# Whitening of a local-attention output: the 128x128 block-diagonal matrices become stacked 64x64 blocks

## The chip, the cores and the metric

The kernel runs on one core of a Trainium2 chip. Its engines work side by side, each through its own queue: TensorE (PE, matrix products; its weight loads are listed as PEld), VectorE (DVE), ScalarE (ACT), GpSimd (POOL), and the DMA queues, most of them issued by SyncE (SP). The metric is the time of one execution in device microseconds (us); lower is better.

## What is computed

The input x has 4 images of 256 channels of 64x64 pixels. The first layer is a local attention: a 7x7 convolution with dilation 2 and a 1x1 convolution give 49 logits for each pixel, a softmax turns them into weights, and each output pixel is the weighted sum of 49 shifted pixels of x. The second layer whitens the result in groups of 64 channels (4 groups; m is 4 x 64 x 64 pixels):

```python
x = jnp.transpose(X, (1, 0, 2, 3)).reshape(g, nc, -1)     # g = 4 groups, nc = 64
mean = x.mean(-1, keepdims=True)
xc = x - mean
Sigma = EPS * I + jnp.einsum('gdm,gem->gde', xc, xc) / m
rTr = (1.0 / jnp.einsum('gii->g', Sigma))[:, None, None]
Sigma_N = Sigma * rTr
P = I
for _ in range(T_ITERS):                                  # 5
    P3 = jnp.einsum('gij,gjk,gkl->gil', P, P, P)
    P = 1.5 * P - 0.5 * jnp.einsum('gij,gjk->gik', P3, Sigma_N)
wm = P * jnp.sqrt(rTr)
xn = jnp.einsum('gde,gem->gdm', wm, xc)                   # then * weight + bias
```

## The kernel before

All data are fp32. The 256 channels are two chunks (cc = 0, 1) of 128 partitions, so each chunk holds two whitening groups of 64 channels (GW = 64), one in partitions 0 to 63, one in 64 to 127.

The long first part, to about 674 us, is convolution and attention. While attention blocks finish, L1093 transposes them, L1101 copies them out and L1114 adds up the moments in the PSUM tile `sig`: for each chunk a 128x65 block whose rows 0 to 63 hold the first group's 64x64 second moments and whose rows 64 to 127 the second group's, with the channel sums in column 64.

Then comes whitening, a Python generator `whiten(cc)` per chunk; the two are stepped in turn, so their instructions alternate. Nothing else is left to do in this time but the output stage, which needs the result. Its steps, by line:

- Head. L1304 makes the mean `mu` from `sig`. L1306 scales the identity by it (`D`), and the product L1308 with `blk`, a 128x128 matrix of ones within each group, spreads the means over rows. L1310 negates mu. L1313 fills S with EPS times the identity (scheduled early, near 579 us), L1317 adds each group's second moments into its diagonal block, one instruction per group, and L1320 subtracts the product of the means. L1320 leaves a nonzero only where `blk` has ones, so S is 128x128 with two 64x64 blocks and zeros elsewhere. L1323 and L1325 take the diagonal of S (`dg`); the product L1327 with `blk` sums it to the trace; L1330 is its reciprocal `rtr`; L1331 scales S; L1335 and L1337 make the first iterate Pm = 1.5 I - 0.5 S. Pm and S lie side by side in the tile `PS`.
- Four iterations. L1342 multiplies Pm with [Pm, S], 256 columns, into PSUM; L1300 evicts the result to `sq` (on ACT for chunk 0, on DVE for chunk 1); L1349 multiplies its two halves (128 columns); L1350 scales Pm by 1.5; L1352 subtracts half the product.
- End. L1357 to L1363 make the output scale from the trace. L1367 multiplies Pm with mu; L1370 and L1371 make the shift; L1376 swaps scale and shift between the two groups' partitions and L1378 copies them out (`abx`).

The matrices are symmetric, and zeros outside the two blocks are carried through every product.

The output stage then applies the matrices: L1429 multiplies a full 128x128 matrix with 512 columns, L1445 multiplies the two diagonal 64x64 blocks (`wm[cc][i, i]`) with 512 columns in quarters of the array, L1396 (ACT) and L1398 (DVE) scale and shift into `out` tiles, and L1433 stores them. Its order on TensorE is kept as written (`pe(...)`); elsewhere a scheduler orders the instructions by priority and data. Semaphores follow from data.

PSUM tiles: `tp()` gives one of three rotating banks; `cv_buf` are two banks that the convolution uses until shortly before the end and that the output stage takes in turn with `apply`.

Of the kernel before, what the change touches and what calls it, by code (L numbers as in the profile page):

```python
# [9 lines left out]
F32 = mybir.dt.float32  # L10
AF = mybir.ActivationFunctionType
ALU = mybir.AluOpType
# [20 lines left out]
def kernel(  # L33
# [29 lines left out]
    nc = tc.nc  # L63
    B, C, H, W = x.shape
    P = 128
    NCC = C // P
# [8 lines left out]
    NPIX = B * H * W  # L75
    GW = 64
    T_ITERS = 5
    EPS = 1e-5
# [24 lines left out]
    def tp():  # L103
        return ps_tp.tile([P, 512], F32, tag="tp", name="tp")


    ident = const.tile([P, P], F32, name="ident")
# [44 lines left out]
    t = tp()  # L152
# [3 lines left out]
    t = tp()  # L156
# [4 lines left out]
    cv_buf = []  # L161
    for k in range(2):
        t = ps_cv.tile([P, 512], F32, name=f"cv{k}")
# [50 lines left out]
    def evict(k, o, i):  # L214
        (nc.vector.tensor_copy if k % 2 else nc.scalar.copy)(o, i)

    for k, c0 in enumerate(range(0, P, CB)):
        n = min(CB, P - c0)
        t = cv_buf[k % 2]
        for cc in range(NCC):  # L220
# [5 lines left out]
                    start=True, stop=True,  # L226
# [8 lines left out]
    for k0 in range(0, KT, TB):  # L235
        n = min(TB, KT - k0)
        t = tp()
# [235 lines left out]
    def col_ops(src, i):  # L473

        X = src.rearrange("p q r c (b a two) -> p (q r c b) a two", a=4, two=2)
        s3 = lambda v: v.rearrange("p (e b) two -> p e b two", b=Q8)
        X4 = [s3(X[:, :, a]) for a in range(4)]
        o = {
            b: xh[b][:, :Q8].rearrange("p q e b two -> p (q e) b two")[:, :, :Q8] for b in ORDER
        }  # L480
        E, O = s3(ct[:, :, 0:2]), s3(ct[:, :, 2:4])
        EO = ct.rearrange("p e (a two) -> p e a two", a=2)
        if i == 0:
            add(EO, X[:, :, 0:2], X[:, :, 2:4])
            yield
            add(o[1], E, O)
            sub(o[2], E, O)
            nc.scalar.copy(o[0], X4[0])
        elif i == 1:
            madd(EO, X[:, :, 2:4], 4.0, X[:, :, 0:2])  # L490
            yield
            madd(o[3], O, 2.0, E)
            madd(o[4], O, -2.0, E)
            nc.scalar.copy(o[INF], X4[3])  # L494
        else:
            madd(o[5], X4[0], 2.0, X4[1])
            yield
            madd(o[5], o[5], 2.0, X4[2])
            yield
            madd(o[5], o[5], 2.0, X4[3])  # L500
# [286 lines left out]
    gs = [col_ops(xr, i) for i in three]  # L787
# [65 lines left out]
    bpool = ctx.enter_context(tc.tile_pool(name="bp", bufs=1, side="right"))  # L853
# [8 lines left out]
    for k in range(NY):  # L862
        a = bpool.tile([P, NCC, P // GW, GW + 1], F32, name=f"yt{k}")
# [95 lines left out]
    back = []  # L959
# [26 lines left out]
    def load_band(n, part):  # L986
# [4 lines left out]
        m0, m1 = BAND[part]  # L991
        D = sd[n % 2][:]
        for g in range(CR):
            dma = nc.sync.dma_start(
                band[g * SW : (g + 1) * SW, m0:m1, g : g + KS].rearrange("p m e w -> p m (e w)"),
                bass.AP(
                    tensor=D.tensor,
                    offset=D.offset + g * SW * DW + m0 * KS * SW + R,
                    ap=[[DW - 1, SW], [KS * SW, m1 - m0], [1, KS * SW]],
# [271 lines left out]
    rpool = ctx.enter_context(tc.tile_pool(name="rp", bufs=1, reuse_waits="tile"))  # L1271
# [6 lines left out]
    blk = rpool.tile([P, P], F32, name="blk")  # L1278
# [9 lines left out]
    finish()  # L1288


    def square(name):
        return bpool.tile([P, P], F32, tag="xb", name=name, bufs=4)

    wm, sc, beta, abx = {}, {}, {}, {}

    def whiten(cc):


        def evict(o, i):
            (nc.vector.tensor_copy if cc else nc.scalar.copy)(o, i)  # L1300

        G = sig[:, cc]
        mu = work.tile([P, 1], F32, tag="mu", name=f"mu{cc}")
        nc.vector.tensor_scalar(mu, G[:, GW : GW + 1], 1.0 / NPIX, None, ALU.mult)  # L1304
        D = square(f"D{cc}")
        nc.vector.tensor_scalar(D, ident, mu, None, ALU.mult)  # L1306
        t = tp()
        nc.tensor.matmul(t[:, :P], blk, D, start=True, stop=True)  # L1308
        nmu = work.tile([P, 1], F32, tag="nmu", name=f"nmu{cc}")
        nc.vector.tensor_scalar(nmu, mu, -1.0, None, ALU.mult)  # L1310
        PS = rpool.tile([P, 2, P], F32, tag="PS", name=f"PS{cc}", bufs=2)
        S = PS[:, 1]
        nc.vector.tensor_scalar(S, ident, EPS, None, ALU.mult)  # L1313
        yield
        for g in range(P // GW):
            gs = slice(g * GW, (g + 1) * GW)
            nc.vector.scalar_tensor_tensor(  # L1317
                S[gs, gs], G[gs, :GW], 1.0 / NPIX, S[gs, gs], ALU.mult, ALU.add
            )
        nc.vector.scalar_tensor_tensor(S, t[:, :P], nmu, S, ALU.mult, ALU.add)  # L1320
        yield
        dt_ = square(f"dt{cc}")
        nc.vector.tensor_tensor(dt_, S, ident, ALU.mult)  # L1323
        dg = work.tile([P, 1], F32, tag="dg", name=f"dg{cc}")
        nc.vector.tensor_reduce(dg, dt_, AX.X, ALU.add)  # L1325
        t = tp()
        nc.tensor.matmul(t[:, :1], blk, dg, start=True, stop=True)  # L1327
        yield
        rtr = work.tile([P, 1], F32, tag="rtr", name=f"rtr{cc}")
        nc.vector.reciprocal(rtr, t[:, :1])  # L1330
        nc.vector.tensor_scalar(S, S, rtr, None, ALU.mult)  # L1331


        i15 = square(f"i15_{cc}")
        nc.vector.tensor_scalar(i15, ident, 1.5, None, ALU.mult)  # L1335
        Pm = PS[:, 0]
        nc.vector.scalar_tensor_tensor(Pm, S, -0.5, i15, ALU.mult, ALU.add)  # L1337
        yield

        for it in range(1, T_ITERS):  # L1340
            t = tp()
            nc.tensor.matmul(  # L1342
                t[:, : 2 * P], Pm, PS.rearrange("p a c -> p (a c)"), start=True, stop=True
            )
            sq = rpool.tile([P, 2, P], F32, tag="sq", name=f"sq{cc}_{it}", bufs=2)
            evict(sq.rearrange("p a c -> p (a c)"), t[:, : 2 * P])
            yield
            t = tp()
            nc.tensor.matmul(t[:, :P], sq[:, 0], sq[:, 1], start=True, stop=True)  # L1349
            nc.vector.tensor_scalar(Pm, Pm, 1.5, None, ALU.mult)  # L1350
            yield
            nc.vector.scalar_tensor_tensor(Pm, t[:, :P], -0.5, Pm, ALU.mult, ALU.add)  # L1352
            yield


        q = work.tile([P, 1], F32, tag="q", name=f"q{cc}")
        nc.scalar.activation(q, rtr, AF.Sqrt)  # L1357
        qi = work.tile([P, 1], F32, tag="qi", name=f"qi{cc}")
        nc.vector.reciprocal(qi, q)
        nc.vector.scalar_tensor_tensor(q, qi, rtr, q, ALU.mult, ALU.add)  # L1360
        ab = work.tile([P, 2], F32, tag="ab", name=f"ab{cc}")
        scale = ab[:, 0:1]
        nc.vector.scalar_tensor_tensor(  # L1363
            scale, q, 0.5, gain_sb[:, cc : cc + 1], ALU.mult, ALU.mult
        )
        t = tp()
        nc.tensor.matmul(t[:, :1], Pm, mu, start=True, stop=True)  # L1367
        yield
        bt = ab[:, 1:2]
        nc.vector.tensor_scalar(bt, t[:, :1], scale, -1.0, ALU.mult, ALU.mult)  # L1370
        nc.vector.tensor_tensor(bt, bt, shift_sb[:, cc : cc + 1], ALU.add)  # L1371
        wm[cc], sc[cc], beta[cc] = Pm, scale, bt
        yield

        t = tp()
        nc.tensor.matmul(t[:, :2], swap, ab, start=True, stop=True)  # L1376
        abx[cc] = work.tile([P, 2], F32, tag="abx", name=f"abx{cc}")
        nc.vector.tensor_copy(abx[cc], t[:, :2])  # L1378

    chains = [whiten(cc) for cc in range(NCC)]  # L1380
    for _ in itertools.zip_longest(*chains):
        pass
# [17 lines left out]
    def two_banks():  # L1400
        while True:
            t = ps_y.tile([P, 2, NT], F32, tag="y", name="apply")
            yield [t[:, k] for k in range(2)]
            yield cv_buf

    G0, G1 = slice(0, GW), slice(GW, P)
    two = two_banks()
    for b in (3, 2, 1, 0):
        for cc in range(NCC):
            for q in range(0, SH // TR, 2):  # L1410
# [30 lines left out]
                for k in range(2):  # L1441
                    for i in (G0, G1):
                        o = i if k == 0 else (G1 if i is G0 else G0)
# [3 lines left out]
                                start=True, stop=True, skip_group_check=True,  # L1447
# [41 lines left out]
```

## Time and profile before

| | us |
|---|---|
| three runs | 745.64, 747.56, 749.41 (median 747.56) |
| the profiled execution | 746.19 |
| span of its instructions | 744.4 |
| mean granted TensorE clock | 0.986 of full speed |

| engine | busy us | share of the span | instructions |
|---|---|---|---|
| PE | 703.4 | 94% | 7512 |
| DVE | 611.3 | 82% | 1268 |
| ACT | 332.5 | 45% | 953 |
| POOL | 51.6 | 7% | 52 |

How to read it: a product of fp32 operands appears as two weight loads and two matmul records, so x4 stands for two products. Ends of matmuls are modelled, so PE counts as busy while it only waits for a result to leave the array; whether it bounds a stretch is seen from what the next engine waits for. "[0.25 <-PE tp L1342]" behind a row says how long its engine stood idle before it and which instruction ended that. A shape 128*64 128x65 is a product with 128 rows and 64 columns of weights and a 128x65 result. PEclk is the TensorE clock that was granted, 1.00 being full speed.

### The profile page before, as it was taken

What the parts mean: (1) busy time and instruction counts of PE and PEld (TensorE: products, weight loads), DVE (VectorE), ACT (ScalarE), POOL (GpSimd) and SP (SyncE); (2) the same over time, 40 slices, a digit from 0 to 9 for tenths busy, and PEclk for the clock granted to TensorE, in tenths of its full rate; (3) what the DMA queues carried; (4) which work ended last, traced back from release to release, by engine and by line L of the source; (5) the groups of instructions that cost most, each with busy time, mean ns of one, the idle gap of its engine ahead of it and who ended that gap; (6) DMA issues with size and microseconds to landing.
All of it is one profiled execution on the core that took longest, in us unless ns stands there. A gap on an engine that the chain in (4) does not pass through costs nothing.

```text
span 744.4 us, 18491 instructions
## 1 busy us (share of the span) xinstructions
PE 703.4 (94%) x7512; PEld 528.3 (71%) x7512; DVE 611.3 (82%) x1268; ACT 332.5 (45%) x953; POOL 51.6 (7%) x52
## 2 busy tenths in 40 slices
PE   6999999997999897999999999999999889998996
PEld 1449543377898794799998958898998678885331
DVE  3789998999999989968995999799969655535575
ACT  1424240255364543466444435735535663322564
POOL 0410070020001110001000100000000000000000
PEclk9999999999899999999999999999999999999999
DMA  8991120147263491076545820534423144371588
GB/s 319 250 319 73 60 88 12 60 147 212 87 193 112 146 317 48 21 245 199 185 128 201 253 69 7 166 108 135 155 64 95 32 149 118 104 296 72 219 357 327
DMA packets 59629, 114.41 MB, mean 154 GB/s; under 512 B 22887, under 2 KB 42008, under 8 KB 58776
## 3 DMA queue, kind: packets, MB, share of 16 engines
q1 hardware_dynamic: 55848, 94.36, 38.7%
q0 software_dynamic: 3696, 18.88, 7.3%
q8 instruction: 59, 0.97, 0.5%
q14 instruction: 26, 0.21, 0.1%
HBM read 65.88 MB, written 47.33 MB: 152 GB/s over the span
## 4 chain that ended last, share of the span: by engine, by line
PE 61%; DVE 28%; ACT 4%; issue 3%; DMA 2%; SPq 0%; DVEq 0%; ACTq 0%
PE cv L538 20%; PE y L1061 12%; PE acc L685 6%; PE tp L1429 4%; PE tp L1093 3%; PE sig L1114 3%; PE cv L685 3%; PE tp L1032 3%; DVE xh L313 3%; DVE pv L313 3%; DVE zz L313 2%; DVE rb L313 2%; PE cv L222 2%; DVE ct L313 2%; DVE band L1009 2%
## 5 line engine op out<-in xcount | busy, mean ns | idle before, releaser
L538 PE MATMUL cv<-xh,wr 128*49 128x128 f32 x4368 | 250.2, 276 | 5.7 <-DVE rm L899 5.3
L538 PEld LDWEIGHTS cv<-xh,wr 128*49 128x49 f32 x4368 | 244.1, 124 | 9.6 <-ACT xh L494 5.5
L1061 PE MATMUL y<-band,xb 128*128 128x224 f32 (+2 forms) x640 | 150.6, 373 | 7.6 <-ACT xb L1040 5.9
L1061 PEld LDWEIGHTS y<-band,xb 128*128 128x128 f32 x640 | 109.1, 192 | 29.0 <-ACT xb L1040 8.9
L548 ACT COPY pv<-cv 113x486 f32<-113x486 f32 (+1 forms) x63 | 30.0, 476 | 86.1 <-PE cv L538 85.8
L1080 ACT ACTIVATE slot<-y,pivot 128x512 f32<-128x512 f32 x53 | 36.6, 738 | 63.5 <-PE y L1061 63.4
L1101 ACT COPY yt<-tp 128x256 f32<-128x256 f32 x128 | 45.6, 378 | 38.8 <-PE tp L1093 37.6
L1032 PE MATMUL tp<-ident,slot 128*128 128x128 f32 x256 | 49.9, 297 | 6.7 <-ACT yt L1101 6.7
L313 DVE SCALAR_TENSOR_TENSOR pv<-pv 113x162 f32<-113x162 f32 x186 | 54.9, 318 | 1.0 <-ACT pv L548 0.4
L1093 PE MATMUL tp<-ident,slot 128*128 128x128 f32 x256 | 52.1, 299 | 3.6 <-ACT yt L1101 1.0
L1009 DVE STREAM_TRANSPOSE band<-band 128x864 f32<-128x864 f32 (+1 forms) x48 | 47.4, 990 | 9.5 <-DMA band<-sd 9.5
L1093 PEld LDWEIGHTS tp<-ident,slot 128*128 128x128 f32 x256 | 41.3, 205 | 13.8 <-issue 4.4
L1032 PEld LDWEIGHTS tp<-ident,slot 128*128 128x128 f32 x256 | 39.9, 205 | 13.0 <-ACT yt L1101 8.0
L941 ACT COPY zt<-d 32x112 f32<-32x112 f32 (+2 forms) x156 | 44.8, 287 | 1.9
L893 ACT ACTIVATE d<-tp,mx 128x49 f32<-128x49 f32 x128 | 37.0, 336 | 17.4 <-DVE mx L888 13.9
L313 DVE SCALAR_TENSOR_TENSOR xh<-ct 128x512 f32<-128x512 f32 x42 | 27.8, 683 | 14.1 <-PE cv L538 13.7
L1114 PE MATMUL sig<-yt 128*64 128x65 f32 x1024 | 36.9, 225 | 0.0
L1114 PEld LDWEIGHTS sig<-yt 128*64 128x64 f32 x1024 | 32.4, 137 | 6.0 <-issue 4.5
L1040 ACT COPY xb<-tp 128x256 f32<-128x256 f32 x87 | 30.5, 376 | 12.9 <-PE tp L1032 12.4
L1040 DVE COPY xb<-tp 128x256 f32<-128x256 f32 x41 | 16.5, 421 | 23.5 <-PE tp L1032 23.5
L685 PE MATMUL acc<-slot,tap 128*49 128x496 f32 (+3 forms) x168 | 34.6, 569 | 0.0
L893 ACT ACTIVATION_READ_ACCUMULATOR d<-tp,mx 128x1 f32 x128 | 30.6, 241 | 0.0
(222 smaller groups left out, 959.2 us busy)
## 6 DMA issues: line engine op xcount, KB each, us to landing
out_dram<-out SPq DMA_DIRECT2D x32, 512.0 KB, 3.4
sd<-zt SPq DMA_DIRECT2D x16, 896.0 KB, 4.2
slot<-in_x_dram POOLq DMA_DIRECT2D x12, 1024.0 KB, 10.0
band<-sd SPq DMA_DIRECT2D x128, 84.0 KB, 2.2
wr<-gd SPq DMA_DIRECT2D x15, 588.0 KB, 3.7
wr<-gd SPq DMA_DIRECT2D x15, 490.0 KB, 3.9
spill<-slot POOLq DMA_DIRECT2D x3, 2048.0 KB, 7.7
back<-spill SPq DMA_DIRECT2D x3, 2048.0 KB, 13.3
```

The lines of the kernel that those rows point to most:

```text
L313: return in_turn(STT(o, a, f, b, ALU.mult, ALU.add))
L538: nc.tensor.matmul(cv[h * HB : h * HB + KT, k, sr : sr + n, sc : sc + n], wv[:, sc, sr, cc], xh[bc][:, :n, h * NCC + cc, :n], start=(j == ...
L685: nc.tensor.matmul(ps[h * HB : h * HB + KT, :, w0:w1_], w[v][:, cc], xs[:, :, cc, w0 + d : w1_ + d], start=(j == 0), stop=(j == len(order) ...
L893: nc.scalar.activation(d[:, h, i], lt[i // NI][:, i % NI, h, :KT], AF.Exp, bias=mx[:, i, h : h + 1], accum_out=s[:, h, i : i + 1],)
L941: ins = nc.scalar.copy(o, i)
L1009: return nc.vector.transpose(f, f)
L1032: nc.tensor.transpose(t[:, cc * P : (cc + 1) * P], xt[:, cc, CR * m : CR * (m + 1), bass.ds(pc, SW, 2)], ident,)
L1040: (nc.vector.tensor_copy if tail else nc.scalar.copy)(xb, t[:, :C])
L1061: nc.tensor.matmul(ps[:, cc, q0 - half * HALF : q1 - half * HALF, :], xb[:, cc * P : (cc + 1) * P], rhs, start=(k == 0), stop=(k == len(PI ...
L1093: nc.tensor.transpose(t[:, cc * P : (cc + 1) * P], yt[:, cc, CR * i : CR * (i + 1), bass.ds(pc, SW, 2)], ident,)
L1101: nc.scalar.copy(yb.rearrange("p a g c -> p (a g) c")[:, :, :GW], t[:, :C].rearrange("p (e c) -> p e c", c=GW),)
L1114: nc.tensor.matmul(sig[g * GW : (g + 1) * GW, cc], yb[:, cc, g, :GW], yb[:, cc, g], start=(count[0] == 0 and cc == 0), stop=(count[0] == 4 ...
```

## The change

The whitening matrices lose their zeros. Each chunk's Pm, S and what goes with them become 128x64 tiles: the first group's 64x64 block in partitions 0 to 63, the second's in 64 to 127. `own` is the identity in that form, `eps` and `i15` are multiples of it, made once.

Each product of the iterations becomes two products of 64x64 weights (`parts_mm`), one per group, in different quarters of the array; for chunk 1 the squares are written to the other half of the partitions (`crossed`) and the second products write them back, so that the two chunks use different quarters. The diagonal for the trace is taken from `sig` directly, with the mean's square subtracted from the sums, and its product with `blk` is issued next to the mean's product, into a bank of `cv_buf`. At the end the two blocks of Pm are copied into a zeroed 128x128 matrix `full[cc]`, which the product with mu and the output stage use. In the changed kernel's own line numbers: L1322 is the eviction and the copy to `full`, L1314 every product of `parts_mm`, L1330 and L1341 the products with `blk`, L1345 and L1346 build S, L1349 the reciprocal, L1354 the first Pm, L1365 and L1367 the update, L1384 the product with mu, L1387 and L1388 the shift, L1393 the swap, L1445 and L1461 the output products.

```diff
-    def square(name):
-        return bpool.tile([P, P], F32, tag="xb", name=name, bufs=4)
+    G0, G1 = slice(0, GW), slice(GW, P)
+
+    def small(name):
+        return rpool.tile([P, GW], F32, name=name)
+
+    own, eps, i15 = small("own"), small("eps"), small("i15")
+    nc.vector.tensor_tensor(own, ident[:, :GW], ident[:, GW:], ALU.add)
+    nc.vector.tensor_scalar(eps, own, EPS, None, ALU.mult)
+    nc.vector.tensor_scalar(i15, own, 1.5, None, ALU.mult)
+    full = []
+    for cc in range(NCC):
+        full.append(rpool.tile([P, P], F32, name=f"full{cc}"))
+        nc.gpsimd.memset(full[cc], 0.0)
+
+    def parts_mm(t, lhs, rhs, crossed, back=False):
+        for i, o in ((G0, G1 if crossed else G0), (G1, G0 if crossed else G1)):
+            if back:
+                i, o = o, i
+            nc.tensor.matmul(
+                t[o], lhs[i], rhs[i], start=True, stop=True, skip_group_check=True
+            )
...
-        D = square(f"D{cc}")
-        nc.vector.tensor_scalar(D, ident, mu, None, ALU.mult)
+        D = small(f"D{cc}")
+        nc.vector.tensor_scalar(D, own, mu, None, ALU.mult)
         t = tp()
-        nc.tensor.matmul(t[:, :P], blk, D, start=True, stop=True)
+        nc.tensor.matmul(t[:, :GW], blk, D, start=True, stop=True)
...
-        PS = rpool.tile([P, 2, P], F32, tag="PS", name=f"PS{cc}", bufs=2)
-        S = PS[:, 1]
-        nc.vector.tensor_scalar(S, ident, EPS, None, ALU.mult)
-        yield
-        for g in range(P // GW):
-            gs = slice(g * GW, (g + 1) * GW)
-            nc.vector.scalar_tensor_tensor(
-                S[gs, gs], G[gs, :GW], 1.0 / NPIX, S[gs, gs], ALU.mult, ALU.add
-            )
-        nc.vector.scalar_tensor_tensor(S, t[:, :P], nmu, S, ALU.mult, ALU.add)
-        yield
-        dt_ = square(f"dt{cc}")
-        nc.vector.tensor_tensor(dt_, S, ident, ALU.mult)
+        dt_ = small(f"dt{cc}")
+        nc.vector.tensor_tensor(dt_, G[:, :GW], own, ALU.mult)
         dg = work.tile([P, 1], F32, tag="dg", name=f"dg{cc}")
         nc.vector.tensor_reduce(dg, dt_, AX.X, ALU.add)
-        t = tp()
-        nc.tensor.matmul(t[:, :1], blk, dg, start=True, stop=True)
+        nc.vector.tensor_scalar(dg, dg, 1.0 / NPIX, EPS, ALU.mult, ALU.add)
+        nc.vector.scalar_tensor_tensor(dg, mu, nmu, dg, ALU.mult, ALU.add)
+        tt = cv_buf[cc]
+        nc.tensor.matmul(tt[:, :1], blk, dg, start=True, stop=True)
+        PS = rpool.tile([P, 2, GW], F32, tag="PS", name=f"PS{cc}", bufs=2)
+        S = PS[:, 1]
+        yield
+        nc.vector.scalar_tensor_tensor(S, G[:, :GW], 1.0 / NPIX, eps, ALU.mult, ALU.add)
+        nc.vector.scalar_tensor_tensor(S, t[:, :GW], nmu, S, ALU.mult, ALU.add)
         yield
         rtr = work.tile([P, 1], F32, tag="rtr", name=f"rtr{cc}")
-        nc.vector.reciprocal(rtr, t[:, :1])
+        nc.vector.reciprocal(rtr, tt[:, :1])
         nc.vector.tensor_scalar(S, S, rtr, None, ALU.mult)
-        i15 = square(f"i15_{cc}")
-        nc.vector.tensor_scalar(i15, ident, 1.5, None, ALU.mult)
...
         for it in range(1, T_ITERS):
             t = tp()
-            nc.tensor.matmul(
-                t[:, : 2 * P], Pm, PS.rearrange("p a c -> p (a c)"), start=True, stop=True
-            )
-            sq = rpool.tile([P, 2, P], F32, tag="sq", name=f"sq{cc}_{it}", bufs=2)
-            evict(sq.rearrange("p a c -> p (a c)"), t[:, : 2 * P])
+            parts_mm(t[:, : 2 * GW], Pm, PS.rearrange("p a c -> p (a c)"), cc)
+            sq = rpool.tile([P, 2, GW], F32, tag="sq", name=f"sq{cc}_{it}", bufs=2)
+            evict(sq.rearrange("p a c -> p (a c)"), t[:, : 2 * GW])
             yield
             t = tp()
-            nc.tensor.matmul(t[:, :P], sq[:, 0], sq[:, 1], start=True, stop=True)
+            parts_mm(t[:, :GW], sq[:, 0], sq[:, 1], cc, True)
             nc.vector.tensor_scalar(Pm, Pm, 1.5, None, ALU.mult)
             yield
-            nc.vector.scalar_tensor_tensor(Pm, t[:, :P], -0.5, Pm, ALU.mult, ALU.add)
+            nc.vector.scalar_tensor_tensor(Pm, t[:, :GW], -0.5, Pm, ALU.mult, ALU.add)
             yield
...
+        for i in (G0, G1):
+            evict(full[cc][i, i], Pm[i])
         t = tp()
-        nc.tensor.matmul(t[:, :1], Pm, mu, start=True, stop=True)
+        nc.tensor.matmul(t[:, :1], full[cc], mu, start=True, stop=True)
...
-        wm[cc], sc[cc], beta[cc] = Pm, scale, bt
+        wm[cc], sc[cc], beta[cc] = full[cc], scale, bt
```

More of the change, by code (lines that the diff above doesn't have):

```diff
@@ L1404, in two_banks @@
             yield cv_buf
-    G0, G1 = slice(0, GW), slice(GW, P)
     two = two_banks()
```

## The prediction

> **What bounds the kernel now.** I read the chain of waits first, around the one place that the change touches. Columns: start (us), length (us), engine, tile, line.
>
> ```profile
> 673.14 1.11 PE sig L1114 x32
> ...
> 674.27 0.22 DVE mu L1304 x2
> ...
> 678.45 1.22 PE tp L1342 x4
> ...
> 688.29 0.40 PE tp L1367 x2
> ...
> 689.66 1.34 PE tp L1429 x2
> ```
>
> The last moments end at 674.22, the first output product starts at 689.52. These 15.3 us are whitening alone, and nothing else runs. They split into a head (674.27 to 678.45, where DVE prepares), four iterations (to 687.76) and an end (to 689.52). Then TensorE is busy without a gap until 736.24, so whatever whitening loses moves the end by as much.
>
> The timeline of the last iteration, chunk 0 (chunk 1 runs half a step behind; columns as above, then tiles and shapes):
>
> ```profile
> 685.67 1.24 PE L1342 MATMUL tp<-PS 128*128 128x256 f32 x4
> 686.41 0.23 DVE L1350 TENSOR_SCALAR PS<-PS 128x128 f32<-128x128 f32 x1 [0.25 <-PE tp L1342]
> 686.46 0.37 ACT L1300 COPY sq<-tp 128x256 f32<-128x256 f32 x1 [1.72 <-PE tp L1342]
> 686.88 1.03 PE L1349 MATMUL tp<-sq 128*128 128x128 f32 x4
> 687.42 0.28 DVE L1352 SCALAR_TENSOR_TENSOR PS<-tp,PS 128x128 f32<-128x128 f32 x1
> 687.76 0.27 PE L1367 MATMUL tp<-mu,PS 128*128 128x1 f32 x1
> ```
>
> It is a latency chain: square 0.79, eviction 0.42, second product 0.54, update 0.34, together 2.09. L1350 ends long before L1352 needs it.
>
> The table by stretches (us, then busy time and count of PE, PEld, DVE, ACT, POOL, then PEclk, the granted clock):
>
> ```profile
> 673.10:676.52 3.42, 1.83 (x37) 1.53 (x36) 2.12 (x13) 1.69 (x3) 0.00 (x0) 1.00 0.05 19
> 676.52:679.93 3.41, 2.22 (x10) 1.49 (x10) 2.88 (x15) 0.68 (x3) 0.00 (x0) 0.99 0.00 0
> 679.93:683.34 3.41, 3.35 (x11) 2.19 (x9) 2.18 (x13) 0.37 (x1) 0.00 (x0) 0.51 0.00 0
> 686.76:690.17 3.41, 2.83 (x15) 1.93 (x14) 1.93 (x10) 0.07 (x1) 0.00 (x0) 0.99 0.00 0
> 690.17:693.58 3.41, 3.41 (x11) 0.81 (x10) 0.59 (x1) 0.78 (x1) 0.00 (x0) 0.51 0.00 0
> ```
>
> Twice here the clock is halved for 3.41 us, each time right after a stretch with little work. The first costs the iterations 9.31 - 4 x 2.09 = 0.95 us; the second lies in the output stage, where PE is the bound, and costs half of 3.41, 1.7 us. So 2.65 us of the profiled execution are clock.
>
> Last, the timelines of DVE in the head and of PE in the output stage:
>
> ```profile
> 675.14 0.47 DVE L1317 SCALAR_TENSOR_TENSOR PS<-sig,PS 64x64 f32<-64x64 f32 x2
> 675.54 0.33 DVE L1320 SCALAR_TENSOR_TENSOR PS<-tp,nmu,PS 128x128 f32<-128x128 f32 x1
> 675.90 0.23 DVE L1317 SCALAR_TENSOR_TENSOR PS<-sig,PS 64x64 f32<-64x64 f32 x1
> 676.16 0.29 DVE L1323 TENSOR_TENSOR dt<-PS,ident 128x128 f32<-128x128 f32 x1
> ```
>
> ```profile
> 698.02 0.66 PE L1445 MATMUL apply<-slot,PS 64*64 64x512 f32 x4
> ```
>
> L1317 works on half the partitions at a time; around it each row starts only when the one before has ended (675.90 after 675.87, 676.16 after 676.13), while elsewhere rows overlap: 0.07 us from start to start for one column (674.27, 674.34), 0.13 for 64 (674.41, 674.54). And the four quarters of the array run four 64x64 products in the time of one.
>
> **The head: -1.4.** Out go four L1317, two L1335 and full-width forms; in come, for each chunk, a diagonal product of sig itself, two one-column rows for the trace, and one sig row at full height (L1345) for two halves. I walk the changed program's DVE order with those spacings, a dependent row starting 0.03 after its input ends. Lengths: one column 0.15, 64 columns 0.21 (L1317: 0.20 to 0.23), L1346 0.27 (L1320's 0.34 less 64 columns). From mu0 at 0: dt0 0.07, D0 0.20, dg0 0.40, mu1 0.53, dt1 0.60, D1 0.80, dg0 complete 1.08, dg1's reduction 1.07 to 1.28, the two L1345 at 1.20 and 1.40, dg1 complete 1.69. Trace product of chunk 1: 1.73, its reciprocal 0.42 later (L1367 at 688.29 to L1370 at 688.72), 2.15. Behind it in DVE's order wait the scalings of S (2.22, 2.35), then Pm0, 2.48 to 2.69; PE at 2.73, against 4.18 now: -1.45. The other bound: the 22 rows before took 4.12 with lengths that sum to 5.41 (76%); the 23 new lengths sum to 4.4, and 76% of that is 3.4: -0.8. I take -1.4, for the half-height rows that spoil the 76% are gone; at best -1.6.
>
> The trace's products queue on PE behind both mean products; that hides behind DVE's L1346 rows. Without that cover it is 0.2.
>
> **The iterations: 4 x -0.57 = -2.3.** Each product becomes two 64x64 ones.
> - Square, 128 columns for 256: L1349 has 128 columns and takes 0.54. The weights are 64 columns wide (L1445 loads in 130 ns, L1349 in 188), -0.05; ACT starts 0.05 after DVE, +0.05. So 0.54 for 0.79, -0.25. Ends: 0.43 (L1367, one column) and 0.75 (0.54 and the second pair streamed in turn: 256 columns at 0.84 ns, from four 320-column L1061 in 1.08 us, 0.21).
> - Eviction: ACT copies of 256, 162 and 98 columns take 372, 291 and 241 ns, so 128 take some 0.265, -0.11; on DVE -0.13 (425 at 256, 559 at 392).
> - Second product, 64 columns: between 0.37 (L1367 less 0.06 for weights) and 0.51 (0.40 and 128 columns in turn, 0.11). I take 0.40, as quarters overlap at L1445: -0.14.
> - Update: 287 ns at 128 columns, 219 at L1317's 64: -0.07.
> The ends are -0.30 and -0.73 an iteration, -1.2 and -2.9 in all.
>
> **The end: +0.4.** Pm must become a full matrix: two 64x64 copies per chunk. For chunk 0 on ACT (L701, 64 columns: 213 ns) they take 0.5 with handoffs, under chunk 1, which is 0.5 behind. For chunk 1 on DVE they are 0.2 each (L953, 64x112: 214 ns), the second after the first as around L1317: 0.43, and L1384 waits. Behind L1384 on PE are the swap products and the first output product, which need it anyway; DVE's L1387 waits for PE too. Ends +0.25 and +0.6.
>
> **Hidden.** PE turns from full products to 64x64 ones ahead of the first L1314 and back at L1384. In the output stage a group of four full and eight quarter pieces takes 2.94 us (1.92 and 1.02 in the chain of waits), while their columns at 0.84 ns make 1.72 + 0.86 = 2.58: at most 0.18 for each turn. At both new turns PE waits for DVE anyway, so I take nothing; without that cover +0.36. Three 128x64 rows (own, eps, i15) stand where two L1313 stood, at 579.5; DVE then idles 1.29 us until 581.12. Without that gap: 0.1. Two memsets of 0.21 go to POOL after 580.0, where its work ends at 580.6 for the rest of the program. No DMA, no other queue, and no order ahead of 674 changes.
>
> **The clock: -0.7.** Array time, at 0.84 ns a column: 676.52 to 679.93 had 1284 columns, 1.08 us or 32%; 686.76 to 690.17 some 35%; both were followed by half clock. 673.10 to 676.52 had 47% (1.12 of moments, 0.43 of L1308, 0.05) and wasn't. The changed iteration has 0.64 us of array time (768 columns) in 1.52, 42%; the moments' stretch 39%. Both lie between, so the rows don't decide. Ends: no half clock any more, -2.65; or half clock through all four iterations (0.5 each by the row pair 0.79 and 0.54, which grew to 1.26 and 0.81 at half clock, scaled to 0.94 us of product: 2.0 for 0.95), +1.05. I take -0.7, near the middle.
>
> [...]
>
> [...]
>
> **Sum.** -1.4 - 2.3 + 0.4 - 0.7 = -4.0 on the profiled 746.19 gives 742.2. That execution lies 1.37 below the median of the runs, 747.56, so against the median: **743.6**.
>
> **Rivals.**
> - The clock stays up throughout. For: array share above 35%. Against: head and end still have 1 to 2 us without products. -3.3 - 2.65: 741.6.
> - Half clock through all iterations. For: shorter products, 39% in the stretch ahead. Against: at half clock the array share doubles, and 679.93 to 683.34 was followed by full clock. -3.3 + 1.05: 745.3.
> - Slower: the 64x64 pieces run one after another, each with its latency. Four at the shortest L1349 piece, 275 ns, make 1.10 for 0.79; four at L1114's 222 make 0.89 for 0.54: +0.66, less 0.18 for eviction and update, +0.48 an iteration, +1.9 in all; with head and end +0.9: 748.5. It decides from 0.2 us more for each product, instead of less. Against it stands the L1445 row.
>
> **Chances.** Within 0.5% (743.8 to 751.3) is what a measurement of this kernel can't tell from no change, and my forecast is on that edge. Forecast 58% (743.6; its own range 742.2 to 745.0): 34 faster, 24 same. Clock up 16%: all faster. Half clock 21%: 1 faster, 20 same. Serial pieces 5%: 3 same, 2 slower. That is 0.51, 0.47, 0.02. All best ends give 740.7, all worst 747.6; leaving out 2 in 10, 741.2 to 746.4.
>
> **What would show it.** Head: first L1314 some 2.7 us after the first mu. Iterations: 1.5 us from square to square at PEclk 1.00, the pieces of a pair starting together. End: two L1322 copies ahead of L1384. Clock: PEclk in the 3.41 us stretches around whitening. I am wrong if pairs run in turn, if the head is still over 3.4, or if anything ahead of the last L1114 moves.

## The result, and the profile after

The changed kernel took 746.07 us in the median of 12 runs (744.25 to 748.64), the kernel before 747.70 in 12 runs beside it: a ratio of 0.9983, 95% interval 0.9971 to 0.9995. By the ratio it is faster by about 1.3 us. Forecast were 743.6 us, 4.0 less than before. The profiled execution took 747.68 us, with a span of 745.9 and a mean clock of 0.98.

The chain of waits of the changed kernel, at the places that the prediction showed (start, length, engine, tile, line):

```profile
676.03 1.11 PE sig L1114 x32
...
690.51 1.92 PE tp L1445 x2
```

The last moments end some 3 us later than in the profile before, which the prediction had named as a sign of being wrong. The change is not the cause: its only instructions ahead of them stand at 582.4 to 583.8 us (L1301 to L1307), and one and the same row of ACT (L893) starts at 312.73 before and at 315.61 here, already 2.9 us later. This execution had half clock near 251 us, which the profile before had not, and two stretches of it in place of one near 285; a second profile of the kernel before, below, has the same. Only distances are compared below. From the end of the moments to the first output product (690.37) there are 13.24 us, where there were 15.30.

The same by stages (head, iterations, end; us, busy time and count of PE, PEld, DVE, ACT, POOL, then PEclk, DMA share, GB/s):

```profile
677.13:680.22 3.09, 1.37 (x9) 1.15 (x9) 3.04 (x24) 0.87 (x2) 0.00 (x0) 1.00 0.01 5
680.22:687.45 7.23, 6.63 (x64) 4.18 (x64) 4.33 (x25) 1.16 (x5) 0.00 (x0) 0.59 0.01 2
687.45:690.37 2.92, 1.86 (x9) 1.80 (x9) 1.39 (x8) 0.48 (x2) 0.00 (x0) 0.50 0.00 0
```

Before, these were 4.23, 9.31 and 1.76 us at PEclk 1.00, 0.82 and 1.00. Head and iterations are shorter, the end is longer, and PEclk is the column to read: the clock is now halved nearly throughout the iterations and in all of the end.

The timeline of the first iteration, which began at full clock, the starts of the squares that follow, and the copies at the end:

```profile
680.22 0.48 PE L1314 MATMUL tp<-PS 64*64 64x128 f32 x8 [0.80 <-DVE PS L1354]
680.69 0.27 ACT L1322 COPY sq<-tp 128x128 f32<-128x128 f32 x1 [1.01 <-PE tp L1314]
...
681.01 0.74 PE L1314 MATMUL tp<-sq 64*64 64x64 f32 x8 [0.31 <-ACT sq L1322]
...
681.43 0.58 DVE L1367 SCALAR_TENSOR_TENSOR PS<-tp,PS 128x64 f32<-128x64 f32 x2
...
681.70 1.06 PE L1314 MATMUL tp<-PS 64*64 64x128 f32 x8
...
683.62 1.03 PE L1314 MATMUL tp<-PS 64*64 64x128 f32 x8
...
685.54 1.01 PE L1314 MATMUL tp<-PS 64*64 64x128 f32 x8
...
687.49 0.50 ACT L1322 COPY full<-PS 64x64 f32<-64x64 f32 x2 [0.89 <-DVE PS L1367]
687.79 0.39 DVE L1322 COPY full<-PS 64x64 f32<-64x64 f32 x2
688.04 0.93 PEld L1384 LDWEIGHTS tp<-mu,full 128*128 128x128 f32 x4 [0.81 <-ACT full L1322]
```

From square to square the first iteration took 1.48 us (680.22 to 681.70), against 2.09 before; the next two took 1.92 each. A row of eight squares lasts 0.48 us at first and over 1.0 once the clock is halved.

The table by stretches of 3.41 us around whitening, as in the prediction:

```profile
677.86:681.28 3.42, 2.01 (x20) 1.44 (x20) 2.92 (x24) 0.57 (x3) 0.00 (x0) 1.00 0.00 0
681.28:684.69 3.41, 3.32 (x31) 2.01 (x28) 2.09 (x13) 0.53 (x2) 0.00 (x0) 0.52 0.02 5
684.69:688.10 3.41, 2.63 (x25) 1.81 (x25) 2.17 (x11) 0.75 (x3) 0.00 (x0) 0.50 0.00 0
688.10:691.52 3.42, 2.95 (x10) 2.22 (x10) 1.03 (x7) 0.00 (x0) 0.00 (x0) 0.50 0.00 0
691.52:694.93 3.41, 3.41 (x11) 0.80 (x10) 0.52 (x1) 0.78 (x1) 0.00 (x0) 0.50 0.00 0
694.93:698.34 3.41, 3.41 (x14) 1.08 (x13) 1.90 (x3) 2.19 (x3) 0.00 (x0) 0.97 0.37 154
```

Half clock lasts four stretches without a break, 13.65 us. The kernel before had one stretch in the iterations, then full clock, then one in the output stage. Of the 13.65 us, 4.56 lie behind 690.37 in the output stage. There a group of eight L1461 products takes 1.92 us in the chain of waits at half clock (692.42) and 1.02 at full clock (696.65), so their cost is put at half, 2.3 us, an estimate; before it was 1.7. Whitening gained 2.06, the output stage lost 0.57: 1.5 us, near the 1.3 measured.

So each profile is summed up here by one figure: whitening plus half of the half-clock time in the output stage. It is 17.0 before and 15.5 after. In the further profiles it is counted to the first output product of the chain of waits (690.51 above) and not to its first record (690.37), which adds up to 0.14 us.

### The profile page after: what moved, and what is told of

It reads as the page before. It is cut to its first block, busy times and chain, and to the rows that moved or that the text cites. A ratio compares the mean times of both kernels' runs of the same rounds, so it can differ in the third digit from the quotient of the medians.

```text
span 745.9 us, 18571 instructions
## 1 busy us (share of the span) xinstructions
PE 704.8 (94%) x7544; PEld 529.3 (71%) x7544; DVE 609.9 (82%) x1271; ACT 332.0 (45%) x955; POOL 50.8 (7%) x54
## 4 chain that ended last, share of the span: by engine, by line
PE 66%; DVE 26%; ACT 5%; issue 2%; DMA 1%; SPq 0%; DVEq 0%; ACTq 0%
PE cv L538 22%; PE y L1061 14%; PE acc L685 6%; PE tp L1445 4%; PE tp L1093 3%; PE sig L1114 3%; PE tp L1032 3%; PE cv L685 3%; DVE xh L313 3%; DVE pv L313 2%; DVE zz L313 2%; PE cv L222 2%; DVE ct L313 2%; DVE ct L306 2%; DVE band L1009 2%
## 5 line engine op out<-in xcount | busy, mean ns | idle before, releaser
L1061 PE MATMUL y<-band,xb 128*128 128x224 f32 (+2 forms) x640 | 154.2, 380 | 8.5 <-ACT xb L1040 6.8
L1061 PEld LDWEIGHTS y<-band,xb 128*128 128x128 f32 x640 | 111.2, 196 | 31.0 <-ACT xb L1040 9.6
L893 ACT ACTIVATE d<-tp,mx 128x49 f32<-128x49 f32 x128 | 37.0, 336 | 17.4 <-DVE mx L888 13.9
L1040 DVE COPY xb<-tp 128x256 f32<-128x256 f32 x41 | 16.5, 422 | 22.8 <-PE tp L1032 22.8
L893 ACT ACTIVATION_READ_ACCUMULATOR d<-tp,mx 128x1 f32 x128 | 30.7, 241 | 0.0
```

The lines of the kernel that those rows point to most:

```text
L893: nc.scalar.activation(d[:, h, i], lt[i // NI][:, i % NI, h, :KT], AF.Exp, bias=mx[:, i, h : h + 1], accum_out=s[:, h, i : i + 1],)
L1040: (nc.vector.tensor_copy if tail else nc.scalar.copy)(xb, t[:, :C])
L1061: nc.tensor.matmul(ps[:, cc, q0 - half * HALF : q1 - half * HALF, :], xb[:, cc * P : (cc + 1) * P], rhs, start=(k == 0), stop=(k == len(PI ...
```

## The experiments

Two theories stood against each other. The first: the new products are as short as forecast, and the halved clock eats the gain. The second: the 64x64 products are slower in themselves inside the iterations. "Fill" below is an unused product of the identity with itself, put into TensorE's waits; it changes no result. `ps_y` is the pool of PSUM tiles that the output stage uses later.

**Fills in the changed kernel.** Full 128x128 products in the waits of the head (2, 1, 4), of each iteration (1, 1) and of the end (3, 1).

```diff
+    idle = ps_y.tile([P, 2, 512], F32, tag="y", name="idle")
+    def fill(n):
+        for k in range(n):
+            pe(nc.tensor.matmul(idle[:, k % 2, :P], ident, ident, start=True, stop=True, ...))
...
             parts_mm(t[:, : 2 * GW], Pm, PS.rearrange("p a c -> p (a c)"), cc)
+            fill(1 * cc)
...
             parts_mm(t[:, :GW], sq[:, 0], sq[:, 1], cc, True)
+            fill(1 * cc if it < T_ITERS - 1 else 3 * cc)
```

> The changed kernel with 128x128 products of the identity, which nothing waits for and whose result is not used, put into TensorE's waits: 2 behind the last moments, 1 and 4 in the head, 2 in each iteration, 3 and 1 in the end. Theory 1 (the clock): the changed whitening leaves the array so idle that the half clock comes in the head and stays; with the products it goes. Then PEclk is 1.00 around whitening, an iteration takes 1.5 us instead of 1.92, the end 2.1 instead of 2.9, the output stage loses 2.3 us less: 4.4 us off, 741.7, ratio to before 0.992. Theory 2 (the forms): the 64x64 products, copies and handoffs are slower than reckoned in themselves; then the added products change nothing or cost: 746 to 748.

Measured: 743.42 us, ratio to before 0.9936 [0.9914, 0.9958]. There is no half clock in the whitening:

```profile
675.79:687.85 12.06, 11.82 (x117) 8.98 (x118) 8.21 (x57) 2.51 (x9) 0.00 (x0) 1.00 0.00 1
```

The figure is 12.06 us.

**Full fills in the kernel before**, in somewhat other numbers (head 2, 5, 1; iterations 1, 1; end 1, 1).

> The kernel before with the same unused products in TensorE's waits (2, 5 and 1 in the head, 2 in each iteration, 2 in the end). Theory 1: the 2.65 us that half clock costs in the profiled execution of before go, so 745.0, ratio 0.9965. Theory 2 says nothing of the clock: 747.7, or later by what the products delay.

Measured: 745.05 us, 0.9967 [0.9938, 0.9996]; again no half clock, and 14.48 us:

```profile
674.18:688.66 14.48, 13.63 (x83) 11.19 (x84) 11.25 (x55) 2.46 (x7) 0.00 (x0) 1.00 0.01 1
```

The kernel before also gains when its clock stays up, but less than the changed one. Counted to the first record, as the 17.0, its own structure takes 14.37 and its half clock 2.6 more; forecast were 2.65.

**Fills in quarters in the changed kernel**: each fill is now a pair of 64x64 products in two quarters of the array. By the gate the expectation means whatever sets the granted clock.

```diff
-            pe(nc.tensor.matmul(idle[:, k % 2, :P], ident, ident, start=True, stop=True, ...))
+            for i in (G0, G1):
+                pe(nc.tensor.matmul(idle[i, k % 2, :P], ident[i, i], ident[i], start=True, stop=True, ...))
```

> As the first run, but each unused product is a pair of 64x64 products in two quarters of the array, as many columns and as long. If the gate counts the time in which anything streams, this equals the first run, 741.7. If it counts how much of the array works, a pair counts half and the clock falls or stays low: PEclk 0.50 in part of the whitening, 743 to 746.

Measured: 742.91 us, 0.9930 [0.9911, 0.9950], the lowest ratio of all, though not to be told from that of the full fills. The windows of head, iterations and end:

```profile
677.16:680.30 3.14, 3.08 (x36) 2.55 (x38) 3.04 (x24) 0.89 (x2) 0.00 (x0) 1.00 0.00 0
680.30:686.30 6.00, 5.40 (x104) 3.47 (x102) 4.37 (x26) 1.16 (x5) 0.00 (x0) 1.00 0.01 3
686.30:688.54 2.24, 1.98 (x21) 1.51 (x18) 1.32 (x8) 0.48 (x2) 0.00 (x0) 1.00 0.00 0
```

PEclk is 1.00 throughout, and the four iterations take 6.00 us although they carry more products (x104 for x64). The figure is 11.38 us. This fells the second theory: at full clock the 64x64 products are as quick as forecast. Pairs that use half of the array held the clock here, at PEclk 1.00 in all three rows, as the full products did in the row of the first run (1.00): the first case of the expectation.

**The early trace alone**, in the kernel before with its 128x128 matrices kept.

```diff
         nc.vector.tensor_scalar(S, ident, EPS, None, ALU.mult)
+        dt_ = rpool.tile([P, GW], F32, name=f"dt{cc}")
+        nc.vector.tensor_tensor(dt_, G[:, :GW], own, ALU.mult)
+        dg = work.tile([P, 1], F32, tag="dg", name=f"dg{cc}")
+        nc.vector.tensor_reduce(dg, dt_, AX.X, ALU.add)
...
+        nc.tensor.matmul(tt[:, :1], blk, dg, start=True, stop=True)
         yield
...
-        dt_ = square(f"dt{cc}")
-        nc.vector.tensor_tensor(dt_, S, ident, ALU.mult)
...
-        nc.vector.reciprocal(rtr, t[:, :1])
+        nc.vector.reciprocal(rtr, tt[:, :1])
```

> The kernel before with one part of the change alone: the diagonal taken from sig and the trace's product issued beside the mean's, all else 128x128. Both theories give the head some 0.5 us less than 4.23 (L1323, L1325 and L1327 leave the chain, two short rows per chunk come). The clock's stretches stay as before by theory 1: 747.2, ratio 0.9993; the rest of the head's gain belongs to the 64-column rows.

Measured: 747.85 us, 1.0007 [0.9974, 1.0040]. The head of this kernel:

```profile
674.48:678.84 4.36, 1.42 (x8) 1.14 (x9) 4.17 (x27) 1.06 (x3) 0.00 (x0) 0.80 0.00 0
```

A miss: it takes 4.36 us for 4.23. (Half clock begins in it, at 677.1, but from there to 678.84 no product runs.) DVE works 4.17 of them, with 27 rows for 23. What the earlier trace saves in waiting it gives back in rows. Half clock then lasts two stretches, not one as before, and full clock comes back inside the iterations; the figure is 18.0. So the head's gain in the changed kernel goes with its rows: 24 in 3.04 us, 0.13 each, for 23 in 4.04, 0.18 each. No run has the narrower rows without the early trace, so that they alone make the gain is argued, not shown.

**Quarter fills in the head alone** (2, 1, 4). What do the iterations do with a clock that is up when they begin?

> The changed kernel with unused pairs of 64x64 identity products in the head alone (two, one and four pairs at its three waits), none in the iterations or the end. Whitening and the time that half clock costs the output stage came to 17.0 us in the kernel before, 15.5 in the changed one and 11.4 with pairs in all waits. If the iterations' own products (some 42% of the array's time) hold the clock up once the head has done so: 1.5 us from square to square in all four, half clock for one stretch after the sparse end only, 3.2 + 6.1 + 2.2 + 1.7 = 13.2, so 744 and a ratio of some 0.995. If 42% is too little: half clock from one 3.41 us stretch into the iterations, two iterations at 1.9, the end and two stretches of the output stage at half clock, some 15.0, so 746 and 0.9975.

Measured: 745.10 us, 0.9947 [0.9913, 0.9981], the first case. The stretches:

```profile
676.80:680.20 3.40, 2.90 (x46) 2.04 (x46) 2.73 (x19) 0.81 (x4) 0.00 (x0) 1.00 0.03 5
680.20:683.65 3.45, 2.69 (x36) 1.67 (x36) 2.44 (x12) 0.59 (x3) 0.00 (x0) 1.00 0.00 0
683.65:687.07 3.42, 2.46 (x14) 1.47 (x18) 1.37 (x9) 0.70 (x3) 0.00 (x0) 1.00 0.00 0
687.07:690.48 3.41, 3.41 (x11) 1.17 (x4) 0.81 (x1) 0.62 (x2) 0.00 (x0) 0.50 0.13 53
```

The second row holds iterations without any fill, and full clock goes on behind it; the sparse end (third row) is followed by one halved stretch in the output stage. Whitening took 11.38 us, all of it at full clock, plus 1.7: 13.1. In this execution, with the head filled, all four iterations ran at full clock; in the changed kernel it fell inside the first of them, behind the unfilled head. The mean clock of the 12 runs goes from 0.982 to 0.991 (0.989 in the profiled one), so others may have had more half clock.

**Quarter fills in the iterations alone** (1, 1).

> The changed kernel with one unused pair of 64x64 identity products at each wait inside the iterations, none in the head or the end. If half clock is set by a stretch with little work and ended by one with much: the head is followed by one halved stretch of 3.41 us, in which the filled iteration keeps the array nearly always busy, so that full clock comes back inside the iterations (the changed kernel had 13.65 us at half clock without a break there); about 0.9 us lost in the iterations, and after the unfilled end once more one stretch in the output stage (1.7). 3.1 + 7.0 + 2.2 + 1.7 = 14.0 against 17.0: 745, a ratio of some 0.996. If half clock, once begun, lasts whatever the work: as the changed kernel, 0.998 or above.

Measured: 745.65 us, 0.9958 [0.9924, 0.9992]. The stretches:

```profile
680.40:683.81 3.41, 2.73 (x36) 2.07 (x36) 2.27 (x17) 0.59 (x4) 0.00 (x0) 0.50 0.02 5
683.81:687.22 3.41, 3.41 (x50) 2.33 (x47) 2.00 (x11) 0.44 (x2) 0.00 (x0) 0.51 0.00 0
687.22:690.63 3.41, 1.93 (x29) 1.49 (x23) 2.01 (x12) 0.75 (x3) 0.00 (x0) 0.99 0.00 0
690.63:694.04 3.41, 3.41 (x11) 0.71 (x10) 0.20 (x2) 0.78 (x1) 0.00 (x0) 0.51 0.00 0
```

Half clock begins behind the head as in the changed kernel, but it ends behind the second stretch, which is filled without a gap (x50). It lasted two stretches where one was expected: the first began with 0.7 us of the head, and PE was busy for 2.73 us of it. The figure is 12.70 + 1.7 = 14.4. So in this run half clock ended behind a stretch with 50 records of products; behind the two stretches of the changed kernel's own iterations, with 31 and 25, it went on.

**The fills in another share** (head 2, 0, 3; iterations 0, 1; end 2, 1).

> The changed kernel with unused pairs of 64x64 identity products in another share: more of them ahead of the trace and in the end, fewer where TensorE is waited for (head two, none and three; iterations none and one; end two and one). If a stretch needs only something above 40% and the products that stand on the path cost their length: no half clock between 674 and 694, 11.1 us for whitening, 742.6 and a ratio of 0.9925, not to be told from the 742.91 of the fuller filling. If the share falls below what is needed, half clock appears in the iterations and the time goes to 744 or more.

Measured: 744.07 us, 0.9941 [0.9902, 0.9980]. The expected 742.6 missed: its head was followed by one halved stretch.

```profile
678.57:681.98 3.41, 2.80 (x36) 2.05 (x37) 2.91 (x24) 0.57 (x3) 0.00 (x0) 1.00 0.00 0
681.98:685.39 3.41, 3.24 (x38) 2.06 (x38) 2.06 (x13) 0.53 (x2) 0.00 (x0) 0.50 0.02 5
```

At 0.84 ns a column (four L1061 of 320 columns in 1.08 us, in the kernel before) the first row has some 1650 columns of products (pairs counted once), 1.39 us or 41%. The unfilled iterations of the kernel with fills in the head have some 1550 in the 3.41 us that end at 683.68, where the clock record has the end of that stretch; that is 38%, and they held the clock. So 38% held the clock in one execution and 41% did not in another. The 12 runs have mean clocks from 0.977 to 0.991, and the profiled one, with 0.986, lies between. The fuller filling had PEclk 1.00 in all of its whitening.

**Both kernels again**, for further profiles.

> The changed kernel once more, for a second profile. If half clock through the iterations belongs to the change: PEclk of 0.5 to 0.6 in the iterations and at the start of the output stage again, some 13.2 us of whitening with 1.9 us from square to square. The extra half clock ahead of whitening (251.2 to 254.6, and two stretches instead of one at 285), which no line of the change touches, should come and go. If half clock in the iterations were an accident of one execution: 1.5 us from square to square this time.

Measured: 746.73 us in its one run. Half clock without a break from 677.50 to 694.56 (five stretches), 1.86, 1.92 and 1.92 us from square to square; the figure is 13.75 + 2.7 = 16.5. Two of the five:

```profile
677.50:680.92 3.42, 2.31 (x26) 1.59 (x25) 2.36 (x17) 0.57 (x3) 0.00 (x0) 0.51 0.02 5
680.92:684.33 3.41, 3.06 (x32) 1.92 (x28) 2.14 (x11) 0.53 (x2) 0.00 (x0) 0.50 0.00 0
```

> The kernel before once more, for a second profile. If full 128x128 products end the half clock inside the iterations wherever the 3.41 us stretches fall: again half clock for at most two stretches between 677 and 688, full clock before the fourth iteration ends, one stretch in the output stage after that, and whitening with the half-clock loss at 16 to 18 us. If the one stretch of the first profile was luck: half clock through all iterations and into the output stage without a break, as the changed kernel had twice (13.65 and some 17 us).

Measured: 751.04 us in its one run.

```profile
681.65:685.06 3.41, 2.87 (x8) 2.02 (x8) 2.03 (x11) 0.50 (x3) 0.00 (x0) 0.50 0.00 0
685.06:688.47 3.41, 3.35 (x11) 2.44 (x11) 1.79 (x10) 0.37 (x1) 0.00 (x0) 0.50 0.03 5
688.47:691.88 3.41, 3.25 (x14) 1.78 (x14) 1.88 (x8) 0.74 (x2) 0.00 (x0) 1.00 0.00 0
```

Two halved stretches, then full clock again with the last two iterations still to come, and one more in the output stage: 16.57 + 1.7 = 18.3, a little above the 16 to 18 foretold. Ahead of whitening this execution of the kernel before has half clock near 251 us and two stretches near 285, as the first profile of the changed kernel.

> The changed kernel a third time. If its iterations at half clock are too sparse to end it: half clock without a break from the head or the first iteration to at least 690, 1.9 us from square to square. If where the stretches fall decides: full clock comes back inside the iterations this time.

Measured: 750.38 us in its one run; half clock without a break from 684.01 to 697.66, 13.37 + 2.2 = 15.6:

```profile
680.60:684.01 3.41, 2.00 (x20) 1.48 (x20) 2.91 (x24) 0.57 (x3) 0.00 (x0) 1.00 0.00 0
684.01:687.42 3.41, 3.41 (x32) 2.06 (x28) 2.13 (x14) 0.50 (x2) 0.00 (x0) 0.51 0.02 5
687.42:690.83 3.41, 2.78 (x27) 1.77 (x25) 2.07 (x11) 0.78 (x4) 0.00 (x0) 0.50 0.00 0
```

In all three profiles of the changed kernel half clock never ended inside the iterations; in both of the kernel before, and in the one with the early trace, it did. The mean clocks of all runs say the same: 0.977 to 0.981 in the 12 of the changed kernel, 0.9795 in the mean, against 0.984 in those of the kernel before beside the experiments. Over 745 us that is, as an estimate, 6 to 7 us more of half clock; the profiles have 14.8 against 8.5 around whitening. From one execution to the next the figure differs by an us or so (15.5, 16.5 and 15.6 after, 17.0 and 18.3 before). The half-clock stretches ahead of whitening differ between executions too, so the single times are not compared.

All together, the figure beside the ratio. "By the figure" is its difference to the mean of the two profiles of before, 17.65; "by the ratio" is (ratio - 1) x 748. The figure comes from one execution, the ratio from many.

| kernel | figure, us | by the figure | by the ratio [95%] |
|---|---|---|---|
| after (mean of three) | 15.9 | -1.8 | -1.3 [-2.2, -0.4] |
| before, early trace | 18.0 | +0.4 | +0.5 [-1.9, +3.0] |
| before, fills | 14.5 | -3.2 | -2.5 [-4.6, -0.3] |
| after, full fills | 12.1 | -5.6 | -4.8 [-6.4, -3.1] |
| after, quarter fills | 11.4 | -6.3 | -5.2 [-6.7, -3.7] |
| after, fills in the head | 13.1 | -4.6 | -4.0 [-6.5, -1.4] |
| after, fills in the iterations | 14.4 | -3.3 | -3.1 [-5.7, -0.6] |
| after, other share | 12.1 | -5.6 | -4.4 [-7.3, -1.5] |

Every difference by the figure lies inside the interval of the runs.

## Why the prediction was wrong

**The step that failed is the clock**: "I take -0.7, near the middle", and with it the sentence that set aside the rival of half clock through all iterations, "at half clock the array share doubles, and 679.93 to 683.34 was followed by full clock". That stretch of the kernel before had some 1620 to 1920 columns, as the products across its ends are counted; at 1.68 ns each (half clock; an estimate, twice the 0.84) they take 80 to 94% of the array's time. The changed iterations at half clock have fewer columns but about the same waits for ACT and DVE: 681.28 to 684.69 had 1504 with every product counted whole (16 x 128 and 15 x 64, two pieces at a time), some 1370 with the ends left out, 67 to 74%. The share rose from 42%, but it did not double, as the iteration went from 1.52 to 1.92 us, and it did not reach the 80 to 94% behind which full clock had come back. The conclusion was drawn from the denser kernel and carried over to the sparser one.

Counted in columns instead of shares, the step fails more plainly. An estimate from the traces of all twelve profiled kernels, for the stretches from about 670 to 702 us (0.84 ns a column at full clock, 1.68 at half, one product behind another, pairs once): half clock followed stretches with at most some 1650 columns, full clock those with at least some 1550 (1650 with the fills in another share, 1550 with those in the head alone), whichever clock the stretch itself ran at. At half clock products take about twice as long (1.92 us for 1.02, the eight L1461 above), and their columns are the same. The 768 columns of a changed iteration make some 1720 a stretch at 1.52 us from square to square, but only some 1370 at 1.92; the 1536 of an iteration before still make some 1720 at half clock (3.05 us, 685.33 to 688.38 in the second profile).

The bracket that the prediction took, 35% to 47%, was too wide: its 47% took the moments' 1.12 us as array time, but their 32 records of 65 columns, which one behind another would make 1.75 us, took 1.11 in the chain. Taken as two at a time, an estimate, they are 0.87 us by columns, which makes 40%.

Its size: at full clock the changed kernel's whitening takes 11.24 us to the first record (11.38 by the chain; the same with fills throughout and in the head alone), so the profiled 15.5 holds 4.3 us of half clock. Before it was 2.65. The term was +1.6, where -0.7 was taken and +1.05 was the worst end. That end left out that half clock here also ran through the end (2.92 us, for 2.10 with fills) and further into the output stage (4.56 us).

- Head: -1.4 forecast, -1.14 measured (3.09 us; 3.08 in both further profiles). Between its ends, -0.8 and -1.6 (the lengths put at 5.41 for the -0.8 sum to 5.12 in the trace, which makes it -0.6). DVE is busy 3.04 of the 3.09 us, so its rows are the bound; the walked order left it some time free. The place named was right, but with 128x128 rows the trace's new place gained nothing (4.36 for 4.23).
- Iterations: 4 x -0.57 forecast. The one iteration at full clock took 1.48 us for the 1.52 foretold: square 0.47, eviction 0.32, second product 0.42, update 0.27. With fills in the head all four ran so: 678.00, 679.55, 681.06, 682.58 are the starts of their evictions. This part is right.
- End: +0.4 forecast; 2.10 us at full clock for 1.76, both to the first record, is +0.3. Two L1322 copies ahead of L1384, on ACT and on DVE, stand in the timeline as foretold.
- Without the clock the terms made -3.3; 15.30 less the 0.95 us of half clock in the iterations is 14.35, and 11.24 for it makes -3.1. The kernel before with fills took 14.37.
- The rivals: half clock through all iterations is what happened, at 745.3 foretold and 746.07 measured. Serial pieces are excluded by the pairs' 0.48 us. A clock that stays up came with the fills alone.

## What to carry to other kernels

Before shortening products in a latency chain, look at the granted clock of the chain. Here less work in the same waits (768 columns an iteration for 1536) came with 13.7 to 17.1 us of half clock around whitening, for 6.8 and 10.2 before, and of the 3.1 us that the change is worth at full clock 1.3 were left. When a share decides such a question, work it out for the changed kernel in the state it would be in, not for the kernel at hand, and count the columns in a stretch: by the estimates above, the changed iteration's share rose at half clock from 42% to 67 to 74%, while its columns in a stretch fell from some 1720 to some 1370. Unused products in TensorE's waits are a cheap test of it: here they turned 0.17% into 0.70%.

## What the runs showed of the hardware

- In the changed kernel half clock came behind a stretch whose longest gap was 0.80 us (behind L1341) and in which products made up 22% of the 3.41 us (677.86 to 681.28, some 900 columns at 0.84 ns). In the kernel before, the longest gap ahead of the half clock at 679.93 was 1.50 us (675.67 to 677.17). Some 38% held the clock in one stretch (fills in the head) and 41% did not in another (fills in another share).
- Half clock ended behind stretches with 80 to 94% (before), 76 to 90% (685.06 to 688.47 in its second profile) and no gap at all (fills in the iterations), not behind those with 67 to 74% and 69 to 76% (the changed iterations, 681.28 to 684.69 and, in the third profile, 684.01 to 687.42); the ranges are for the products across the ends, and the shares are estimates at 1.68 ns a column. So as a share of the array's time, 38% held a clock that was up, and up to 76% did not bring back one that was down. As columns in a stretch the two lie close together, by the estimate above at some 1550 to 1650.
- With fills in all waits PEclk was 1.00 throughout the changed whitening, with pairs of 64x64 products (11.38 us) as with full 128x128 ones (12.06 us). Some 1550 columns in pairs alone held the clock (the iterations with fills in the head), while some 1230 to 1280 in full products did not (before, 676.52 to 679.93).
